# k and q of a linear attention: sixteen 128x512 matmuls a block replaced by seven products of 128x256 matmuls that share a PSUM bank

## The chip, the cores and the metric

The kernel runs on one core of a Trainium2 chip. The time is device microseconds of one execution, and the number compared is the median of several. TensorE is called PE below, its weight loads PEld, VectorE DVE, ScalarE ACT, GpSimd POOL and SyncE SP; "L217" is line 217 of the kernel before.

## What is computed

Two post-norm layers over x of (2, 1024, 512) in fp32, each with an attention and a feed-forward part, every part followed by a residual add and a layer norm. The change touches the first part alone:

```python
q = feature_map(proj(Wq))            # feature_map(y) = elu(y) + 1, 16 heads of 32
k = feature_map(proj(Wk))
v = proj(Wv)
kv = einsum('bhtd,bhte->bhde', k, v)
z = 1.0 / (einsum('bhtd,bhd->bht', q, k.sum(axis=2)) + 1e-06)
out = einsum('bhtd,bhde,bht->bhte', q, kv, z)
out = out.reshape(b, t, c) @ Wo.T
x = layernorm(x + out)
```

After it come a feed-forward part with weights unpacked from four bits, a gated linear attention in chunks, and a feed-forward part over the 512 best-ranked tokens of each batch.

## The kernel before, in words

The 2048 tokens are four blocks of 512 (two a batch), each of four tiles of 128 rows. x lies in SBUF twice: row by row (`x_t`, four tiles a block) and transposed (`xT`, three rooms that the blocks take in turn, loaded from a transposed copy in HBM). The four weight matrices lie in rooms A0 to A3 (`place_w`). PSUM is eight banks in two rings, "mm" (banks 0 to 3) and "acc" (4 to 7).

The first stage is the loop over `b` at L279. For each of the eight tiles of a batch, `project` (L214) makes k with four matmuls of 128x512, one per 128 input channels, into one bank; `elu1` (L266) turns it into elu + 1 with two ACT instructions and one DVE instruction that reads the bank (L269 to L271); POOL adds k up to `ksum` (L294, L296); and `add_xk` (L284) adds x'k of the tile to four accumulating banks with four matmuls (L286). For the very first block the four tiles are made side by side in all four "mm" banks (L303), because their operands are still arriving. So v is never formed: after the batch, Wv is applied to x'k (L338), the heads are cut out (L340), and Wo is applied (L347), which gives G, a 512x512 matrix. `ksum` is spread over the partitions with a matmul of ones (L330).

The second half of the loop makes q tile by tile in the same way (`new_q`), weighs it with z on DVE (`weigh`, L354 to L360: a product, a sum per head, an add, a reciprocal and a product), turns it with four transposes (L197) and ACT's copy (L365), multiplies it by G (`ao`, L217), adds it to x on DVE (L383) and takes the row statistics (L188, L189). The layer norm of a block runs on POOL (L181, L183). In the second batch the first block's x is meanwhile turned and split into two fp32r parts for the next stage (`split_quarter`, L211 and L212).

Between these steps stand 27 unpacking jobs (`unpack_some`): a load on SP, two integer instructions on DVE (L237, L238) and one conversion on ACT or DVE. Their loads use two buffers. The program order of the instructions on each engine is the order of the calls, moved a little by a scheduler; `tc.issue_after` ties an instruction behind another. Each engine works its queue in order.

The next stage (feed-forward, L471 for gate and up, L518 for the product with the unpacked matrix) starts with `gatep` at L471. L518 there already makes a product of block matrices from seven products of 128x256 matmuls.

Of the kernel before, what the change touches and what calls it, by code (L numbers as in the profile page):

```python
# [21 lines left out]
P = 128  # L22
B, T, C = 2, 1024, 512
NB = 4
# [49 lines left out]
def body(ctx: ExitStack, tc: tile.TileContext, a: dict, out: bass.AP):  # L74
# [8 lines left out]
    dram = ctx.enter_context(tc.tile_pool(name="dram", bufs=1, space=DRAM))  # L83


    rings, turn_of = {"mm": range(4), "acc": range(4, 8)}, {"mm": 0, "acc": 0}

    def bank(ring, name):
        i = rings[ring][turn_of[ring] % len(rings[ring])]
# [3 lines left out]
    def mm_bank(name):  # L93
        return bank("mm", name)
# [25 lines left out]
        return xtp.tile([P, KC, 512], dtype, tag=f"xT{i}", name=name)  # L120

    def new_xT(blk):
        t = xT_slot(blk % 3, f"x0T{blk}")
        return t, a["xT"][:, blk * 512 : (blk + 1) * 512].rearrange("(k p) t -> p k t", p=P)

    def load_xT(blk):
# [35 lines left out]
    wqk = cpool.tile([P, KC, 64], F32, name="wqk")  # L162

    def load_rest():
        xT[2] = load_xT(2)
        load_x(2)
        load_x(3)
        nc.sync.dma_start(out=gus, in_=a["gus"].rearrange("k (f p) -> (k f) p", p=P))
        nc.sync.dma_start(out=gw, in_=a["gw"])
        nc.sync.dma_start(out=b1, in_=a["b1"])  # L170
        nc.sync.dma_start(out=rb, in_=a["rb"].to_broadcast([P, 1]))
        nc.sync.dma_start(out=wqk[:, :, 0:32], in_=a["W1qT"].rearrange("(k p) o -> p k o", p=P))
        nc.sync.dma_start(out=wqk[:, :, 32:64], in_=a["W1kT"].rearrange("(k p) o -> p k o", p=P))
# [16 lines left out]

    last_turned = [None]

    def transposed(x, name):

        pt = mm_bank(name)
        for k in range(KC):
            ins = nc.tensor.transpose(pt[:, k * P : (k + 1) * P], x[:, k * P : (k + 1) * P], ident).ins  # L197
        last_turned[0] = ins
        return pt

    def split_tiles(blk):

        i, j = ((1, 1), (2, 0), (0, 2), (1, 1))[blk]
        hi = xT_slot(i, "x1Th", F32R)
        lo = wpool.tile([P, KC, 512], F32R, tag=f"A{j}", name="x1Tl")
        return hi, lo

    def split_quarter(parts, blk, i):
        hi, lo = (t[:, :, i * P : (i + 1) * P] for t in parts)
        pt = transposed(x_t[blk][:, i], "x1Tp").rearrange("p (k t) -> p k t", k=KC)  # L210
        nc.scalar.copy(hi, pt)  # L211
        nc.vector.tensor_sub(lo, pt, hi.bitcast(F32))  # L212

# [33 lines left out]
    def unpacking():  # L247
        n = 704
        for j in range(2 * I_FF // n):
            cut = slice(j * n, (j + 1) * n)  # L250
            for g in range(KC):
                yield wgu[:, g, cut], a["gu"][16 * g : 16 * (g + 1), cut], None, n
        for g in range(NI):
            yield wdn[:, g], a["dn"][16 * g : 16 * (g + 1), :], a["dns"][g : g + 1, :], C

    to_unpack = unpacking()
# [9 lines left out]
    def elu1(dst, ps):  # L266

        e = wk.tile([P, C], F32, tag="e", name="e")
        nc.scalar.activation(e, ps, AF.Relu, scale=-1.0)  # L269
        nc.scalar.activation(e, e, AF.Exp, scale=-1.0)  # L270
        anchor[0] = nc.vector.scalar_tensor_tensor(dst, ps, 0.0, e, ALU.max, ALU.add).ins  # L271

    ones = wk.tile([P, P], F32, name="ones", bufs=1)
    nc.gpsimd.memset(ones, 1.0)
    xk = wdn[:, NI - KC :]
    tile_of = lambda i: slice((i % 4) * P, (i % 4 + 1) * P)
    for b in range(B):  # L279
        acc = [acc_bank(f"xk{b}_{c}") for c in range(KC)]  # L280
        ksum = wk.tile([P, C], F32, tag="ksum", name="ksum", bufs=1)
        got = []

        def add_xk(i, k):  # L284
            for c in range(KC):
                nc.tensor.matmul(  # L286
                    acc[c], x_t[2 * b + i // 4][:, i % 4, c * P : (c + 1) * P], k, start=i == 0, stop=i == 7
                )

        def keys(i, kp):  # L290
            k = wk.tile([P, C], F32, tag="kq", name="k", bufs=5)
            elu1(k, kp)
            if i == 0:
                nc.gpsimd.tensor_copy(ksum, k)  # L294
            else:
                nc.gpsimd.tensor_add(ksum, ksum, k)  # L296
            return i, k

        if b == 0:
            first = [mm_bank("kp") for _ in range(4)]  # L300
            for k in range(KC):
                for i in range(4):
                    nc.tensor.matmul(first[i], xT[0][:, k, tile_of(i)], Wk[:, k], start=k == 0, stop=k == KC - 1)  # L303
            got = [keys(i, first[i]) for i in range(4)]
        for i in range(4 if b == 0 else 0, 8):
            kp = mm_bank("kp")
            project(kp, xT[2 * b + i // 4][:, :, tile_of(i)], Wk)
            for _ in range(max(1, len(got) - 2)):
                if got:
                    add_xk(*got.pop(0))  # L310
            got.append(keys(i, kp))
            unpack_some((i - 4 if i > 5 else 0) if b == 0 else 2 if i < 7 else 0)
            if b == 0 and i == 4:
                load_rest()
        for p in got:
            add_xk(*p)
        for c in range(KC):
            (nc.scalar.copy if c % 2 else nc.vector.tensor_copy)(xk[:, c], acc[c])

        def new_q(n):  # L320

            qp = mm_bank("qp")
            project(qp, xT[2 * b + n // 4][:, :, tile_of(n)], Wq)
            q = wk.tile([P, C], F32, tag="kq", name="q", bufs=5)
            elu1(q, qp)
            return q

        q = {n: new_q(n) for n in range(2)}
        sp_ = mm_bank("ksumb")
        nc.tensor.matmul(sp_, ones, ksum, start=True, stop=True)  # L330
        ks = wk.tile([P, C], F32, tag="ks", name="ks", bufs=1)
        nc.scalar.copy(ks, sp_)
        G = wk.tile([P, KC, C], F32, tag="G", name="G", bufs=1)
        vk = mm_bank("vk")
        for c in range(KC):
            cut = slice(c * P, (c + 1) * P)
            for k in range(KC):
                nc.tensor.matmul(vk[:, cut], Wv[:, k, cut], xk[:, k, cut], start=k == 0, stop=k == KC - 1)  # L338
        vkm = wk.tile([P, KC, P], F32, tag="vkm", name="vkm", bufs=1)
        nc.vector.tensor_mul(  # L340
            vkm,
            vk.rearrange("p (c d) -> p c d", c=KC),
            const("heads")[:, :P].unsqueeze(1).to_broadcast([P, KC, P]),
        )
        for c in range(KC):
            gp = acc_bank("gp")
            nc.tensor.matmul(gp, vkm[:, c], Wo[:, c], start=True, stop=True)  # L347
            (nc.scalar.copy if c % 2 else nc.vector.tensor_copy)(G[:, c], gp)

        def weigh(n):  # L350

            x = q[n]
            e = wk.tile([P, C], F32, tag="e", name="qk")
            nc.vector.tensor_mul(e, x, ks)  # L354
            z = sp.tile([P, 16], F32, tag="z", name="z", bufs=2)
            nc.vector.tensor_reduce(z, e.rearrange("p (h d) -> p h d", d=32), AX.X, ALU.add)
            nc.vector.tensor_scalar_add(z, z, 1e-6)
            nc.vector.reciprocal(z, z)
            x3 = x.rearrange("p (h d) -> p h d", d=32)
            return nc.vector.tensor_mul(x3, x3, z.unsqueeze(2).to_broadcast([P, 16, 32])).ins  # L360

        def turned(n):
            pt = transposed(q.pop(n), "qTp")
            t = wk.tile([P, KC, P], F32, tag="qT", name="qT")
            nc.scalar.copy(t.rearrange("p k t -> p (k t)"), pt)  # L365
            return t

        mv, qT = {}, {}
        for n in range(10):
            if n < 8:  # L370
                weighed = weigh(n)
            if n + 2 < 8:
                with tc.issue_after(weighed):
                    q[n + 2] = new_q(n + 2)
            if n >= 1 and n <= 8:
                i = n - 1
                blk = 2 * b + i // 4
                if i % 4 == 0:
                    mv = sp.tile([P, 4, 2], F32, tag="mv", name="mv")
                ao = acc_bank("ao")  # L380
                project(ao, qT.pop(i), G)
                x = x_t[blk][:, i % 4]
                nc.vector.tensor_add(x, ao, x)  # L383
                row_stats(mv[:, i % 4], x)
                if i == 7 and b == 1:
                    late = mv
                elif i % 4 == 3:
                    layernorm(x_t[blk], mv, by=nc.gpsimd)
                unpack_some(b or i % 2)
            if n < 8:  # L390
                qT[n] = turned(n)
            if b == 1 and n in (2, 3, 4, 5):
                if n == 2:
                    parts = split_tiles(0)
                split_quarter(parts, 0, n - 2)
            if b == 0 and n == 7:
                xT[3] = load_xT(3)
    unpack_some(1000)
    sg = wk.tile([KC * FG, P], F32, name="sg", bufs=1)
    nc.gpsimd.tensor_copy(sg, gus)  # L400
# [11 lines left out]

    free = iter([2, 1, 0] * 4)

    def xT_tile(name):
        return xT_slot(next(free), name)
# [24 lines left out]
    with tc.tile_pool(name="s2", bufs=1) as wk2:  # L443
# [43 lines left out]
        class Hidden:  # L487


            def __init__(self, blk):  # L490
                i, j = ((0, 2), (1, 1), (2, 0), (0, 2))[blk]
                self.rooms = xT_slot(i, "h"), place_w(j, "h"), extra[blk % 2]

            def chunk(self, f):
# [147 lines left out]
        for blk in range(NB):  # L642
# [45 lines left out]
            pieces = down(h, now.room)  # L688
            if blk > 0:
                old_steps = old.steps()  # L690
        Wog = place_w(1, "Wog")
        load_w(Wog, "WogT")
        rings["mm"], rings["acc"] = range(4), range(4, 8)
        with tc.issue_after(st):
# [9 lines left out]
        now.squares(range(4))  # L704
        now.power()
        ending = now.rest()
        W1o = place_w(2, "W1o")
    fp4.close()


# [713 lines left out]
```

## Time and profile before

| what | us |
|---|---|
| median of 3 runs | 1005.13 (1004.5 to 1005.25) |
| profiled execution, its own time | 1003.83 |
| its span, first to last instruction | 1002.0 |
| first matmul | 4.61 |
| first matmul of the next stage (L471) | 252.61 |
| busy PE, DVE, ACT, POOL over the span | 983.1, 644.6, 274.7, 299.2 |

The mean granted TensorE clock is 0.998 of full speed. The groups of the first stage that the change touches, each 128x512: a matmul pass (L217, L286) has a record of 592 ns, of which 429 ns pass until the next one; a weight load takes 190 ns; L269 takes 591 ns, L270 630, L271 690, L354 699, L356 682, L360 686, L383 686, L188 692, L365 584, and POOL's L296 1291 and L183 2211. To read it: a chain of waits shows which engine the end hangs on; an engine's busy share over the whole run says little about one stage, so the views are asked by stretch of time.

### The profile page before, as it was taken

To read this page: it belongs to the slowest core of one execution; us is meant where nothing else is said; L and a number is where in the kernel's file an instruction comes from. 1 tells how busy PE (TensorE), PEld (TensorE's weight loads), DVE (VectorE), ACT (ScalarE), POOL (GpSimd) and SP (SyncE) were. 2 spreads that over 40 slices of the span, in tenths; PEclk is the share of its full clock that TensorE was granted. 3 is DMA by queue.
4 is the path that set the end of the run, shared out by engine and by line. 5 is a ranking of instruction groups with operands and counts; after the bars stand their busy time and mean duration, and the time that the engine had idled before them with its cause. 6 is when DMAs were issued, how large, how long until landed. Compare 5 with 4: busy or idle time off the path is not lost.

```text
span 1002.0 us, 10997 instructions
## 1 busy us (share of the span) xinstructions
PE 983.1 (98%) x4061; PEld 708.8 (71%) x4061; DVE 644.6 (64%) x1233; ACT 274.7 (27%) x466; POOL 299.2 (30%) x277
## 2 busy tenths in 40 slices
PE   8999999999999999999999999999999999999996
PEld 3454444544788888888889765676778688888885
DVE  1236754476996576676664366656698795689644
ACT  2223222223463245245231333132220124220000
POOL 2100452004577536566557011201023002000022
PEclk9999999999999999999999999999999999999999
DMA  9611123100000000000011320000003402140011
GB/s 345 208 50 57 43 58 111 36 32 0 1 1 1 1 1 1 0 1 11 1 43 43 120 101 1 0 1 1 0 16 125 143 17 80 43 168 1 1 42 43
DMA packets 25689, 48.82 MB, mean 49 GB/s; under 512 B 4652, under 2 KB 6316, under 8 KB 25123
## 3 DMA queue, kind: packets, MB, share of 16 engines
q1 hardware_dynamic: 22995, 42.85, 13.0%
q0 software_dynamic: 1920, 4.22, 1.1%
q10 hardware_dynamic: 720, 1.05, 0.3%
q8 instruction: 32, 0.52, 0.2%
q14 instruction: 22, 0.18, 0.1%
HBM read 39.70 MB, written 10.52 MB: 50 GB/s over the span
## 4 chain that ended last, share of the span: by engine, by line
PE 84%; issue 8%; DVE 4%; POOL 2%; ACT 1%; DMA 0%; POOLq 0%; DVEq 0%; ACTq 0%
PE P L518 12%; PE yp L1168 9%; PE hp L1089 9%; PE upp L471 8%; PE gatep L471 8%; PE qp L217 5%; PE xk L286 5%; PE ao L217 5%; PE kp L217 4%; PE ao L972 3%; PE go L928 2%; PE lp L434 1%; PE kp L303 1%; PE P L527 1%; PE up L845 1%
## 5 line engine op out<-in xcount | busy, mean ns | idle before, releaser
L181 POOL TENSOR_TENSOR rs<-rs,table 128x4 f32<-128x4 f32 (+1 forms) x21 | 19.6, 936 | 324.2 <-DVE rs L180 323.9
L482 DVE SCALAR_TENSOR_TENSOR gate<-gatep,scale,gate 128x512 f32<-128x512 f32 x123 | 91.3, 742 | 7.3 <-PE gatep L471 6.7
L482 DVE SCALAR_TENSOR_TENSOR up<-upp,scale,up 128x512 f32<-128x512 f32 x112 | 83.0, 741 | 0.2
L471 PE MATMUL gatep<-x1Th,wgu 128*128 128x512 f32 x176 | 73.0, 415 | 0.0
L471 PE MATMUL upp<-x1Th,wgu 128*128 128x512 f32 x176 | 69.8, 397 | 0.0
L471 PE MATMUL gatep<-x1Tl,wgu 128*128 128x512 f32 x176 | 69.6, 395 | 0.0
L471 PE MATMUL upp<-x1Tl,wgu 128*128 128x512 f32 x176 | 69.5, 395 | 0.0
L671 POOL TENSOR_TENSOR h<-up,gate 128x512 f32<-128x512 f32 x30 | 38.6, 1286 | 78.3 <-ACT gate L670 73.3
L518 PE MATMUL P<-wdn,h 128*128 128x256 f32 x256 | 60.5, 379 | 0.0
L476 ACT ACTIVATE gate<-gatep,scale 128x512 f32<-128x512 f32 x41 | 28.3, 690 | 113.9 <-PE gatep L471 106.6
L217 PE MATMUL ao<-G,qT 128*128 128x512 f32 x128 | 57.5, 594 | 0.2 <-ACT qT L365 0.2
L217 PE MATMUL qp<-Wq,x0T 128*128 128x512 f32 x128 | 57.6, 592 | 0.0
L286 PE MATMUL xk<-k,x 128*128 128x512 f32 x128 | 56.7, 592 | 0.0
L972 PE MATMUL ao<-W1o,uT 128*128 128x512 f32 x128 | 55.6, 592 | 0.0
L518 PEld LDWEIGHTS P<-wdn,h 128*128 128x128 f32 x256 | 48.5, 190 | 6.7
L876 POOL TENSOR_TENSOR sum<-sum,sq 128x512 f32<-128x512 f32 x12 | 18.2, 1515 | 107.6 <-issue 83.7
L286 PEld LDWEIGHTS xk<-k,x 128*128 128x128 f32 x128 | 24.3, 190 | 30.6 <-issue 30.1
L217 PEld LDWEIGHTS ao<-G,qT 128*128 128x128 f32 x128 | 24.1, 190 | 30.4 <-issue 28.9
L972 PEld LDWEIGHTS ao<-W1o,uT 128*128 128x128 f32 x128 | 24.0, 190 | 28.7 <-issue 27.5
L271 DVE SCALAR_TENSOR_TENSOR k<-kp,e 128x512 f32<-128x512 f32 x16 | 11.0, 690 | 51.1 <-ACT e L270 47.2
L217 PE MATMUL kp<-Wk,x0T 128*128 128x512 f32 x96 | 43.4, 593 | 0.2 <-DVE k L271 0.2
L188 DVE BATCH_NORM_STATS2 st<-x 128x6 f32<-128x512 f32 x64 | 42.8, 682 | 0.8
(348 smaller groups left out, 2130.3 us busy)
## 6 DMA issues: line engine op xcount, KB each, us to landing
pk<-in_gu SPq DMA_DIRECT2D x16, 352.0 KB, 3.8
x<-in_x SPq DMA_DIRECT2D x4, 1024.0 KB, 12.7
w<-in_w SPq DMA_DIRECT2D x1, 4096.0 KB, 14.4
xs<-picked SPq DMA_DIRECT2D x4, 1024.0 KB, 5.2
out<-x SPq DMA_DIRECT2D x4, 1024.0 KB, 4.5
w<-in_w SPq DMA_DIRECT2D x4, 1024.0 KB, 6.6
x0T<-in_xT SPq DMA_DIRECT2D x3, 1024.0 KB, 8.7
pk<-in_dn SPq DMA_DIRECT2D x11, 256.0 KB, 3.6
```

What stands on the lines that cost most here:

```text
L188: nc.vector.bn_stats(st, x)
L217: nc.tensor.matmul(ps, lhs[:, k], w[:, k], start=start and k == 0, stop=stop and k == KC - 1)
L286: nc.tensor.matmul(acc[c], x_t[2 * b + i // 4][:, i % 4, c * P : (c + 1) * P], k, start=i == 0, stop=i == 7)
L471: ins = nc.tensor.matmul(ps, wgu[:, k, at * P : (at + 1) * P], x[:, k], start=x is parts[0], stop=x is parts[1]).ins
L476: nc.scalar.activation(acc, ps, AF.Copy, scale=s)
L482: last = nc.vector.scalar_tensor_tensor(acc, ps, s, acc, ALU.mult, ALU.add).ins
L518: last_p[0] = nc.tensor.matmul(cut, x(j)[:, r], w[:, j], start=j == 0, stop=j == NP - 1 and tail is None).ins
L671: hm = nc.gpsimd.tensor_mul(h.chunk(f), up, gate).ins
L928: nc.tensor.matmul(ps[:, 256 * m : 256 * m + 256], w[:, k, m], b[:, k, 256 * half : 256 * half + 256], start=k == 0, stop=k == KC - 1,)
L972: nc.tensor.matmul(ao[i], uT[blk][:, k, i * P : (i + 1) * P], W1o[:, k], start=n == 0, stop=n == 3)
L1089: nc.tensor.matmul(ps[:, 256 * j : 256 * j + 256], w[:, k, 2 * g + j], x[:, k], start=k == 0, stop=k == 1)
L1168: nc.tensor.matmul(ps[:, 256 * r : 256 * r + 256], x(r, j), w(j), start=j == 0, stop=j == NJ - 1)
```

## The change

For all blocks but the first, k is no longer made tile by tile. The block's transposed x (512 channels x 512 tokens) and the weights (512 x 512) are each taken as two by two blocks, and seven products of 256x256 blocks, each of four matmuls of 128x256, give the result (`by_seven`). Four sums of x blocks (S1 to S3, and S2 a second time) and, once per weight matrix, four sums of weight blocks (T1 to T4) are made on DVE. q is made so for all four blocks.

Four of the seven products (P1, S2 T2, S1 T1, S2 B22) go one after another into the same bank, "grow", and add up there. After each, ACT copies the bank as it stands into a part of the result, or elu reads it; the next of them is made when that is done. Two more (P7, A22 T4) share a second bank in the same way, read by DVE adds. P2 has a bank of its own. elu is applied to parts of 128x2x256, three of them from SBUF and one from PSUM.

What comes between the products is written out by hand: `run` takes a list of steps for each stop (`yield`). In the stops of k and q of one block stand x'k of the block before, the spreading of ksum, Wv and Wo, the transposes, ao and unpacking jobs of others. `behind()` ties each matmul group behind the one issued before it.

Rooms change with it: xT has two rooms instead of three for x (the third holds sums); the sums also use rw, b2, three slices of the not yet unpacked `wdn` and later Wk's room; x'k and G share one tile; the "mm" ring has banks 0 and 1 from the second block on, "grow" takes 2 and 3 in turn; transposes of q and of the split take "acc" banks. xT of block 2 is loaded after q of block 0 instead of early. In the later stages only the numbers of the rooms are exchanged.

```diff
+    def sums_of_weights(w, rooms):
+        B11, B12, B21, B22 = (w[:, 2 * e : 2 * e + 2, 256 * o : 256 * o + 256] for e in range(2) for o in range(2))
+        T1, T2, T4 = rooms
+        for dst, x, y in ((T1, B12, B11), (T2, B22, T1), (T4, B21, T2), (B12, B22, B12)):
+            nc.vector.tensor_sub(dst, x, y)
+        return T1, T2, B12, T4
+    def by_seven(x, w, T, rooms, pairs, ready):
...
+        def product(ps, a, b, first):
+            with behind():
+                for r in range(2):
+                    for k in range(2):
+                        ins = nc.tensor.matmul(
+                            ps[:, 256 * r : 256 * r + 256], a[:, k, r * P : (r + 1) * P], b[:, k],
+                            start=first and r == 0 and k == 0, stop=k == 1, skip_group_check=True,
+                        ).ins
+            last_pe[0] = ins
+            return ps.rearrange("p (r c) -> p r c", r=2)
+        nc.vector.tensor_add(S1, A21, A22)
+        nc.vector.tensor_sub(S2, S1, A11)
+        nc.vector.tensor_sub(S3, A11, A21)
...
+        grow = bank("sum", "grow")
+        p = product(grow, A11, B11, True)
+        nc.scalar.copy(c11, p)
+        yield
+        p2 = product(mm_bank("P2"), A12, B21, True)
+        nc.vector.tensor_add(c11, c11, p2)
+        elu1(c11, c11)
+        yield
+        product(grow, S2, T2, False)
+        nc.scalar.copy(c21, p)
+        side = mm_bank("P7")
+        p7 = product(side, S3, T3, True)
+        nc.vector.tensor_sub(S2, A12, S2)
+        yield
+        product(grow, S1, T1, False)
+        nc.scalar.copy(c22, p)
+        nc.vector.tensor_add(c22, c22, p7)
+        elu1(c22, c22)
+        yield
+        product(grow, S2, B22, False)
+        elu1(c12, p)
+        ready(0)
+        product(side, A22, T4, False)
+        nc.vector.tensor_add(c21, c21, p7)
+        elu1(c21, c21)
+        ready(1)
...
+    rings["mm"], rings["sum"] = (0, 1), (2, 3)
+    Ts = {"k": sums_of_weights(Wk, slices(Tk, 0, 3))}
+    for i in range(4):
+        elu1(pairs_of["k", 0][i // 2][:, i % 2], first[i])
...
+    for b in range(B):
+        i, j = 2 * b, 2 * b + 1
+        if b:
+            run(
+                k_products(i),
+                turns(1, 0, 1),
+                some_o(1, 0) + turns(1, 2) + job(1) + some_o(1, 1) + turns(1, 3) + job(1),
+                some_o(1, 2) + job(1), some_o(1, 3) + job(1), job(2),
+            )
+        run(k_products(j), [], some_xk(i, 0, 1) + job(2), some_xk(i, 2) + job(1), some_xk(i, 3) + job(1), job(1 + b))
+        if b == 0:
+            Ts["q"] = sums_of_weights(Wq, slices(wdn, 0, 3))
+        else:
...
+            Tq = place_w(1, "Tq")
+            for n in range(3):
+                nc.scalar.copy(Tq[:, n], wdn[:, n])
...
+        run(
+            q_products(i), [],
+            some_xk(j, 0, 1) + job(1), some_xk(j, 2) + step(spread_ksum, b) + job(1), some_xk(j, 3) + job(1 + b),
+        )
+        if b == 0:
+            xT[2] = load_xT(2)
+        split = [step(split_some, n) if b else [] for n in range(4)]
+        run(
+            q_products(j),
+            step(values, b),
+            turns(i, 0, 1) + job(1 - b),
+            step(G_rows, b) + split[0] + job(1 - b),
+            some_o(i, 0) + turns(i, 2) + split[1] + some_o(i, 1) + turns(i, 3) + job(1 - b),
+            some_o(i, 2) + split[2] + some_o(i, 3),
+        )
+        if b == 0:
+            xT[3] = load_xT(3)
+    for more in turns(3, 0, 1) + split[3] + some_o(3, 0) + turns(3, 2) + some_o(3, 1) + turns(3, 3) + some_o(3, 2, 3):
+        more()
```

The methods named in the lists (`add_xk`, `weigh`, `turned`, `add_o`, `spread_ksum`, `split_quarter`) do what their namesakes did before, for the tile given.

## The prediction, made before the changed kernel ran

> **What bounds the kernel now.** I read the page first, then the busy time by stretch, the chain of waits, and last the groups and the order in time.
>
> ```profile
> span 1002.0 us, 10997 instructions
> PE 983.1 (98%) x4061; PEld 708.8 (71%) x4061; DVE 644.6 (64%) x1233; ACT 274.7 (27%) x466; POOL 299.2 (30%) x277
> ...
> PE 84%; issue 8%; DVE 4%; POOL 2%; ACT 1%; DMA 0%; POOLq 0%; DVEq 0%; ACTq 0%
> ```
>
> PE carries the span. The changed stage is the first quarter; its two ends by stretch (columns: stretch, length, then busy us of PE, PEld, DVE, ACT, POOL, then granted clock, DMA share, GB/s):
>
> ```profile
> 118.00:184.00 66.00, 66.00 (x160) 29.38 (x159) 35.60 (x65) 17.46 (x28) 23.94 (x15) 1.00 0.31 88
> 184.00:202.00 18.00, 18.00 (x67) 9.77 (x66) 7.47 (x14) 4.68 (x8) 0.00 (x0) 1.00 0.00 1
> 202.00:253.00 51.00, 50.84 (x156) 24.92 (x154) 35.03 (x75) 15.31 (x27) 10.15 (x5) 1.00 0.05 16
> ```
>
> PE has no holes at full clock; DVE is 54% to 69% busy, ACT has room. So PE time taken out of this stage shortens the run, as far as DVE can follow. The chain (start, us, what) gives the prices:
>
> ```profile
> 4.61 13.84 PE kp L303 x28
> 18.46 0.60 ACT e L269
> 19.06 0.53 ACT e L270
> 19.61 0.70 DVE k L271
> 20.36 3.70 PE kp L217 x8
> ...
> 30.92 3.43 PE kp L217 x8
> ...
> 303.47 6.47 PE P L518 x30
> ```
>
> Each matmul has two records (fp32 takes two passes). Four 128x512 matmuls take 3.43 us, 0.429 a record. L518, in the next stage, already runs the new form, 128x256 on 128x128 weights: 6.47/30 = 0.216 a record.
>
> **The products.** A block of 512 tokens was 16 matmuls of 128x512: 4 x 3.43 = 13.7 us. It becomes 28 of 128x256: 56 x 0.216 = 12.1. Seven blocks change (k of blocks 1 to 3, q of 0 to 3; k of block 0 stays): 7 x 1.64 = **11.5 us less PE**. x'k, ao, the transposes, L330, L338 and L347 keep their number and size and only move.
>
> Here a rule speaks against the change. The Trainium skill ("TensorE: Matmul & The Clock Gate", section Back-to-back issue gap) says that in a stream of weight load and matmul pairs the spacing depends on both, and gives 81 ns at 128 columns and 131 at 512. Halfway in columns between, an estimate from that page, 256 would cost about 98 ns, 0.75 of a 512: a block would be 28 x 0.75 = 21 old matmuls against 16, seven blocks 30 us dearer. The row says 0.216/0.429 = 0.50, because the 190 ns weight load of L518 still fits under its 216 ns pass. I take the row; it is the same shape.
>
> **Price 1, the start.** Block 0's k still fills four banks and ends where it did (same loads, same L303). Before, the next matmul needs the first bank and starts at 20.36, behind one DVE k. Now the growing bank is the third of those four, so PE waits for the third elu. That one is in the trace:
>
> ```profile
> 20.40 0.60 ACT L269 ACTIVATE e<-kp 128x512 f32<-128x512 f32 x1 [0.30 <-DVE k L271]
> ...
> 21.03 0.63 ACT L270 ACTIVATE e<-e 128x512 f32<-128x512 f32 x1
> ...
> 21.69 0.69 DVE L271 SCALAR_TENSOR_TENSOR k<-kp,e 128x512 f32<-128x512 f32 x1 [0.79 <-ACT e L270]
> ```
>
> It ends at 22.38, so PE starts at 22.42: **+2.1 us**. The four sums of Wk and three of xT stand ahead of these elus in DVE's queue. They cost nothing: DVE is idle to 19.61, and block 1's xT, issued at 5.61 with 8.7 us to landing, is there at 14.3, plus three sums = 16.4. Had it landed at the 14.2 us that another xT took, the start would slip by about 2 more. Wq's four sums (2.4 us of DVE) come behind the third elu and delay only the first c11, which has 20 us.
>
> **Price 2, DVE and the stops.** Each of the seven blocks adds four sums of x and three adds of a product on DVE, three bank copies on ACT (7 x 3 x 0.59 = 12 us, in ACT's idle time). The elus keep their number; three of four read SBUF now. 49 DVE instructions more, at what spacing?
>
> ```profile
> 232.68 0.68 DVE L383 TENSOR_TENSOR x<-ao,x 128x512 f32<-128x512 f32 x1
> 233.28 0.68 DVE L360 TENSOR_TENSOR q<-q,z 128x512 f32<-128x512 f32 x1
> 233.88 0.69 DVE L188 BATCH_NORM_STATS2 st<-x 128x6 f32<-128x512 f32 x1
> 234.48 0.67 DVE L212 TENSOR_TENSOR x1Tl<-x1Tp,x1Th 128x512 fp32r<-128x512 f32 x1
> ...
> 235.35 0.68 DVE L354 TENSOR_TENSOR qk<-q,ks 128x512 f32<-128x512 f32 x1
> 236.07 0.69 DVE L356 TENSOR_REDUCE z<-qk 128x16 f32<-128x512 f32 x1
> ```
>
> Independent instructions follow each other in 0.60 us, though one takes 0.68; where one needs its forerunner it is 0.72. A 128x16 one takes 0.10 to 0.15 between others. 49 x 0.60 = 29 us more DVE in 230, so it holds PE only where it comes in a burst: the weighing of q.
>
> Inside a block the waits that the change adds (each product into the growing bank waits for ACT's copy of the one before; behind it in PE's queue stands all else) are covered: the copy is ready 0.2 + 0.59 us after its product, and between stand another product (1.73) and mostly x'k or ao (3.43). Without that cover each would show about 0.8 us.
>
> At q of blocks 0 and 2 the transposes of q follow the last product by 1.73 (side product) + 1.73 (next P1) + 3.57 (vk) + 1.73 (P2) = 8.8 us. The chain behind the growing bank's last product is 0.2 hand-over, 0.60 + 0.63 ACT and hand-overs, so DVE starts at 1.5; elu, p7 add, two mul, two reduce, a sum of x, elu, mul, mul, with a next qk between, are 11 at 0.60, and some small ones: both tiles done at 8.7. Just covered, 0 to 1 us. Block 1 has two ao on top, 10.3 us.
>
> The tail (q of block 3) has no next block. Clock from the end of the growing bank's last product. PE: side 1.73, ao 3.43, transposes 0.44, ao 3.43, two q transposes 0.88, pg 0.08: at 9.99 it wants the last transposes for the split. Their bank is the one that the split before them used, freed by its DVE subtraction (L212). That stands in DVE's queue behind 16 full instructions (elu, p7 add, four of weighing, two mul, elu, x add, four of weighing, stats, mul) and nine small ones: 1.5 + 16 x 0.60 + 1.1 + its own 0.69 = 12.9. PE stalls 12.95 - 9.99 = 2.96, and all of block 3's ao and the next stage are queued behind. The next ao needs a bank that DVE frees 0.75 later: **+3.7 us**. The 0.2 us that ao waits for ACT there now goes.
>
> In the middle the 0.4 us that the transposes wait for DVE at 117.60 goes (block 2's first product stands there, ao beside it); I allow 0.5 for new small waits, between 0 and 1.5.
>
> The skill also bears on DVE ("SBUF — State Buffer", Who interferes with whom): a DVE instruction with two SBUF inputs contends with a GpSimd one that reads SBUF, and the second blocks for the whole of the first. That is what the 28 x sums and 21 of the elus become.
>
> ```profile
> L354 DVE TENSOR_TENSOR qk<-q,ks x16: 656/680/1096, 70.7 to 239.0; 128x512 f32<-128x512 f32 x16
> ```
>
> L354 has two SBUF inputs. At 118.07 it took 1.10 us beside GpSimd's normalization; at 238.95, beside the same 2.1 us instructions, 0.69. One in 16 paid 0.4. By the rule, with GpSimd 50 us busy of 233, about 10 of 49 would wait 1 us: 10 us of DVE, mostly in the k stretches, and perhaps 3.5 on PE. By the row it is 49 x 0.03 = 1.3 us of DVE, within my allowance; in the tail GpSimd is idle. I take the row.
>
> **Queues.** xT of block 2 moves from the early loads to behind q of block 0, as block 3's sits behind q of block 1. PE frees the room at about 75, SP issues then, and with 8.7 us it lands at 84, with 14.2 at 89; DVE first reads it at about 89 to 92. Covered; if not, DVE's queue stops there and PE about 3 us later. Unpacking loads behind it on SP have two buffers and the same cover. GpSimd keeps its work. The three copies of the weight sums (ACT, 1.8 us) run in x'k stops.
>
> **The sum.** -11.5 + 2.1 + (3.7 - 0.2) + (0.5 - 0.4) = -5.8 us. The following stages are PE-bound with rooms only renamed, so it reaches the end. The profiled execution took 1003.83 us with 1002.0 span: 998.0 and 996.2. The median of runs is 1005.13, 1.3 above it: **999.3 us**. About 0.2% (2 us) is what a measurement here can tell from no change.
>
> **Rivals.**
> *No tail stall* (14%): DVE drains faster, or records overstate its hand-overs. -11.5 - 0.6 + 2.1 + 0.5 = -9.5: 995.6. Against: the tail needs 3 us less from 11.
> *GpSimd lock* (14%): as the rule above, -5.8 + 3.5: 1002.8. For: the 1.10 us. Against: the 0.69.
> *DVE becomes the bound, slower* (9%): one mechanism, DVE spacing in the q chains. At 0.75 instead of 0.60 (small ones 0.08 more) the tail is 3.7 + 16 x 0.15 + 9 x 0.08 = 6.8, blocks 0 and 2 lose their 0.5 slack and 1.4 each, and the G copies, x adds and transposes queued behind lose about 1 at each of four places: 2.1 + 6.8 + 2.8 + 4 - 0.6 = 15.1 against 11.5, +3.6: 1008.7. It decides from about 0.71 on; most of this work is dependent, at 0.72, which speaks for it, but pairs of tiles alternate in the queue, which gives 0.60.
> *The products don't pay* (3%): the skill's 98 ns, up to 1035. Against: L518.
>
> My forecast has 60%, 997 to 1001.5. Faster by over 0.2% (below 1003.1): forecast, no tail, and half of the lock, 0.81; slower: DVE's bound and the products, 0.12; 0.07 between. The range leaves out the products, the slower case and the fastest tip: 995.5 to 1004.
>
> **What would show it.** Right: grow and P products at 0.216 a record, 12.1 us a block; first grow at 22.4; one PE gap of about 3 us before the last split transposes, released by DVE, and one under 1 us at the next ao; the gate products start at 252.61 - 5.8, about 246.8. Wrong: gaps ahead of grow products released by ACT; DVE idle under 10% from q of block 2 on; 128x256 records over 0.23 apart; the gate products early but the end not.

## The result, and the profile after

| | before | after |
|---|---|---|
| median (lowest to highest) of 6 runs, us | 1004.68 (1003.83 to 1005.25) | 999.14 (997.57 to 1001.8) |
| ratio, 95% interval | | 0.995 [0.9933, 0.9968] |
| profiled execution: own time, span | 1003.83, 1002.0 | 998.07, 996.3 |
| mean granted clock | 0.998 | 0.996 |
| first matmul; first one after block 0's k | 4.61; 20.36 | 4.57; 22.84 |
| first gate product, and from there to the end | 252.61; 749.4 | 246.72; 749.5 |

The forecast was 999.3. The whole gain lies ahead of the gate products. The runs of after lie three times as far apart as those of before, which asks for a reason as well. ("After" is the changed kernel; "before", "after" and the names of the runs also stand for their profiles.)

The page of the kernel after, the same three lines:

```profile
span 996.3 us, 11402 instructions
PE 972.5 (98%) x4229; PEld 741.8 (74%) x4229; DVE 681.1 (68%) x1290; ACT 288.7 (29%) x490; POOL 302.6 (30%) x277
...
PE 83%; issue 8%; DVE 5%; POOL 2%; ACT 2%; DMA 0%; POOLq 0%; DVEq 0%; ACTq 0%
```

PE lost 10.6 us of busy time with 168 records more; the span lost only 5.7. The difference has to be idle PE. Busy time by stretch (stretch, length, then busy us of PE, PEld, DVE, ACT and POOL, granted clock, DMA share, GB/s):

```profile
20.50:62.00 41.50, 39.20 (x135) 25.48 (x135) 24.32 (x36) 16.52 (x27) 10.81 (x9) 1.00 0.58 182
62.00:118.00 56.00, 56.00 (x224) 37.38 (x223) 42.35 (x88) 21.61 (x36) 1.57 (x2) 1.00 0.23 71
118.00:184.00 66.00, 66.00 (x228) 42.42 (x227) 46.41 (x75) 21.20 (x35) 30.35 (x17) 1.00 0.26 79
184.00:202.00 18.00, 18.00 (x97) 14.96 (x96) 17.40 (x38) 8.14 (x14) 0.00 (x0) 1.00 0.00 0
202.00:247.00 45.00, 41.74 (x138) 22.68 (x136) 26.61 (x55) 12.67 (x23) 9.28 (x5) 0.96 0.00 1
```

From 62 to 202 PE has no hole, though DVE is 97% busy in the 18 us of the fourth row. All idle time is in the first and the last stretch, and in the last the mean granted clock is 0.96; in before it stays at 1.00 from 20 us on until the last 5 us of the program. The start, in the chain:

```profile
4.57 14.28 PE kp L467 x28
...
20.02 0.70 DVE k L272
...
22.10 0.70 DVE k L272
22.80 0.04 issue
22.84 1.99 PE grow L311 x8
24.84 1.73 PE P L311 x8
```

The first growing product waits for the third elu, as forecast. A product then takes 1.73 us for eight records, 0.216 each. The tail, PE in order of time (start, us, instructions in a row, and in brackets the idle time with its releaser):

```profile
226.87 0.24 PE L552 MATMUL pg<-table,sg 88*128 88x88 f32 x1
229.74 0.66 PE L196 MATMUL x1Tp<-table,x 128*128 128x128 f32 x4 [2.63 <-DVE x1Tl L211]
231.03 5.08 PE L440 MATMUL ao<-G,qT 128*128 128x512 f32 x8 [0.63 <-ACT x1Th L210]
235.94 0.60 PE L196 MATMUL qTp<-table,pair 128*128 128x128 f32 x4
236.38 3.60 PE L440 MATMUL ao<-G,qT 128*128 128x512 f32 x8
```

Two waits in the places named, 2.63 and 0.63 us. But the ao behind them takes 5.08 us where the next one takes 3.60. The same time in stretches shows why:

```profile
227.03:230.45 3.42, 0.73 (x6) 0.42 (x4) 3.42 (x11) 2.31 (x6) 0.00 (x0) 1.00 0.00 0
230.45:233.86 3.41, 2.83 (x4) 1.31 (x5) 2.07 (x5) 0.57 (x1) 1.02 (x1) 0.50 0.00 0
233.86:237.27 3.41, 3.41 (x13) 1.69 (x12) 1.09 (x2) 0.59 (x1) 3.31 (x3) 1.00 0.00 0
```

The granted clock is 0.50 for 3.41 us behind the hole, and 1.00 again after that. Such a stretch is called a low stretch below. The price of the tail therefore has a part that the prediction lacks. Theory for the experiments: products 11.5 us cheaper, less one wait at each end, and each wait can bring a lowered clock on top. Rivals: the waits are not what costs (DVE or the GpSimd lock holds PE generally), or the products gain less and something unseen makes it up.

### The profile page after: what moved, and what is told of

Read it like the earlier page. It is cut to its first block, busy times and chain, and to the rows that moved or that the text cites. A ratio compares the mean times of both kernels' runs of the same rounds, so it can differ in the third digit from the quotient of the medians.

```text
span 996.3 us, 11402 instructions
## 1 busy us (share of the span) xinstructions
PE 972.5 (98%) x4229; PEld 741.8 (74%) x4229; DVE 681.1 (68%) x1290; ACT 288.7 (29%) x490; POOL 302.6 (30%) x277
## 4 chain that ended last, share of the span: by engine, by line
PE 83%; issue 8%; DVE 5%; POOL 2%; ACT 2%; DMA 0%; POOLq 0%; DVEq 0%; ACTq 0%
PE P L668 12%; PE yp L1318 9%; PE hp L1239 9%; PE gatep L621 8%; PE upp L621 8%; PE xk L362 6%; PE ao L440 5%; PE grow L311 5%; PE P L311 3%; PE ao L1122 3%; PE go L1078 2%; PE kp L467 1%; PE lp L584 1%; PE P L677 1%; PE up L995 1%
## 5 line engine op out<-in xcount | busy, mean ns | idle before, releaser
L362 PE MATMUL xk<-pair,x 128*128 128x512 f32 x96 | 42.7, 592 | 0.0
L621 PEld LDWEIGHTS upp<-x1Th,wgu 128*128 128x128 f32 x176 | 33.0, 188 | 9.3 <-DVE up L632 1.1
L621 PEld LDWEIGHTS gatep<-x1Th,wgu 128*128 128x128 f32 x176 | 33.1, 188 | 7.7 <-PE x1Tp L196 0.3
L621 PEld LDWEIGHTS upp<-x1Tl,wgu 128*128 128x128 f32 x176 | 33.1, 188 | 7.5
L621 PEld LDWEIGHTS gatep<-x1Tl,wgu 128*128 128x128 f32 x176 | 33.1, 188 | 7.2 <-issue 0.2
```

The lines of the kernel that those rows point to most:

```text
L362: ins = nc.tensor.matmul(acc_of[b][c], x_t[blk][:, i, c * P : (c + 1) * P], pairs_of["k", blk][i // 2][:, i % 2], start=blk % 2 == 0 and i ...
L621: ins = nc.tensor.matmul(ps, wgu[:, k, at * P : (at + 1) * P], x[:, k], start=x is parts[0], stop=x is parts[1]).ins
```

## The experiments

**The tail's bank.** The last two split transposes take a bank of the "mm" ring, so they no longer wait for the subtraction that frees theirs.

```diff
-                split_quarter(parts, 0, i, acc_bank)
+                split_quarter(parts, 0, i, mm_bank if i > 1 else acc_bank)
```

> The last two split transposes take a bank of the other ring (0, 1), so nothing at the end of q of block 3 waits for a bank that DVE has to free. In the changed kernel PE stood idle there 2.63 and 0.63 us, and the ao matmuls after it took 5.08 us in place of 3.43 at a granted clock of 0.53 to 0.61. Theory (a bank wait, and a lower clock because PE stood still): both waits and the slow ao go, -2.6 -0.6 -1.6 = -4.9 us, gate products at about 241.8, run 994.3; the runs lie closer together, with a mean clock of 0.998 in all. Rival (DVE's load at the end is what binds, the bank only shows it): PE waits at the q transposes or at the next ao instead, gain under 1.5 us.

Measured 993.04 us (992.94 to 995.93), ratio to before 0.9884 [0.9868, 0.9901]: 6.1 below the median of after, where 4.9 was expected. The tail's waits are gone, and the ao there takes 3.67 us. One of the four runs, the profiled one, took 2.9 us more than the others, and shows a reason; PE at the start:

```profile
23.80 3.57 PE L311 MATMUL grow<-Wk,x0T 128*128 128x256 f32 x8 [2.30 <-DVE k L272]
27.16 2.05 PE L311 MATMUL P<-Wk,x0T 128*128 128x256 f32 x8
```

The same product after the same 2.30 us wait took 1.99 us in the profile of after. Here the clock fell (0.50 from 24.06 to 27.47), there it did not. So the start's hole lowers the clock in some executions. That makes 1.7 of the 2.9 us, half of the 3.41; block 0's k also ended late in this run (21.51, in after 20.55), and when it ended in the other three is not on record. The mean clock tells the low stretches of runs without a profile, since one takes 0.0017 off it (1.7 of 996 us; an estimate, since the program's end takes another 0.0017 to 0.003 in the profiles): the other three runs here have 0.998 and so none. Every run of after has at least one: three have a mean of 0.996, which makes one low stretch (997.57 to 998.71 us), one 0.995, one or two (999.58), and two 0.993, three (1001.75 and 1001.8). That is how far the runs of after spread.

**The start's banks.** The first growing product gets the bank that block 0's first tile frees.

```diff
-    rings["mm"], rings["sum"] = (0, 1), (2, 3)
+    rings["mm"], rings["sum"] = (2, 3), (0, 1)
```

> The growing banks are 0 and 1, the side banks 2 and 3, so the first product after block 0's k needs the first elu and not the third. Theory: first grow starts near 20.8 and not 22.84; P2 then waits some 0.3 us for the third elu; gain 1.7 to 2.0 us, run 997.3. Rival (PE is held by something later in the first x'k anyway, or DVE falls behind by as much): grow early, but the gap reappears before the first x'k or S2 T2, gain under 0.5 us.

Measured 995.26 us (994.93 to 997.91), ratio 0.9905 [0.9889, 0.9922]: 3.9 below the median of after, more than expected. The wait at the start is 0.21 us and the tail is untouched:

```profile
21.33 1.99 PE L311 MATMUL grow<-Wk,x0T 128*128 128x256 f32 x8 [0.21 <-DVE k L272]
...
228.59 1.12 PE L196 MATMUL x1Tp<-table,x 128*128 128x128 f32 x4 [2.63 <-DVE x1Tl L211]
229.88 6.24 PE L440 MATMUL ao<-G,qT 128*128 128x512 f32 x8 [0.17 <-DVE x L448]
```

The wait is worth 2.1. The rest of the 3.9 is the clock: the other three runs have a mean of 0.998, so no low stretch at all, although the tail's wait is untouched by the edit. The profiled run has two in a row in the tail (6.24 and 1.12 us instead of 5.08 and 0.66), and took 2.4 to 3.0 us more than the other three. So the hole in the tail does not always lower the clock either.

**Both.** The two edits together.

> Both changes of banks together: growing banks 0 and 1 from the start, the last two split transposes in the other ring. Theory (two PE gaps of 2.3 and 2.6 us, each of which can also lower the clock for about 3 us): relative to the tail change alone (993.0) the start gap of 2.1 us and the chance of a clock drop there (1.7 us in some runs) go: 990 to 991, granted clock 0.998, runs within 1 us of each other. Rival (gains share a cause and don't add): 992 to 993.

Measured 991.48 us (991.24 to 992.21), ratio 0.987 [0.9853, 0.9886], between the two expectations; the runs agree within 1 us again, at a mean clock of 0.997 to 0.998. It beats both kernels. All waits of PE from 20 us to the gate products (us in total, times, longest):

```profile
PE grow L311 <- DVE k L272: 0.2, 1, 0.2
```

That also answers where the other 7.7 us of after went: about 1.6 for the start's wait (the step from the tail's edit to both; the rows had 2.1, and why it is less stays open), 3.3 for the tail's two waits, and the remainder of 2.8 for the clock. The mean clocks agree: one to three low stretches a run, on average 1.7 or 1.8, at 1.7 us each are about 3.0.

**Work in the hole.** To separate the wait from the clock: three 128x512 matmuls of ones with ksum, whose results nobody reads, stand ahead of the last split transposes of after. They delay nothing while PE would wait anyway.

```diff
+    def warm():
+        with behind():
+            for _ in range(3):
+                last_pe[0] = nc.tensor.matmul(mm_bank("warm"), ones, ksum_of[1], start=True, stop=True).ins
...
-    for more in turns(3, 0, 1) + split[3] + ...
+    for more in turns(3, 0, 1) + [warm] + split[3] + ...
```

> Three matmuls of 128x512 that nobody reads (ones by ksum) are put where PE waits for the last split transposes; the wait for the bank stays. Theory that the idle PE lowers its clock: the granted clock stays at 1.00 and the next ao takes 3.43 us in place of 5.08, while the transposes start where they did (229.7): about -1.6 us, run 997.5. Rival (ao is slow for its operands or for what ACT and DVE do beside it): ao keeps 5.08 us, time as the changed kernel or up to 0.5 more.

Measured 998.81 us (996.39 to 998.97), ratio 0.9934 [0.9918, 0.9951]: not told apart from after in the total. The rows of PE decide it:

```profile
228.83 2.74 PE L548 MATMUL warm<-ksum,ones 128*128 128x512 f32 x6
231.41 0.24 PE L557 MATMUL pg<-table,sg 88*128 88x88 f32 x1
231.71 0.66 PE L196 MATMUL x1Tp<-table,x 128*128 128x128 f32 x4
...
233.37 3.60 PE L440 MATMUL ao<-G,qT 128*128 128x512 f32 x8
```

With PE at work the same ao takes 3.60 us, so the 5.08 was the clock and not the memory, the bank or the trace. The total did not show it because three of the four runs still have one low stretch by their mean clock (0.996); in the profiled one it lies at the start (the first growing product took 3.54 us). The fourth has 0.998 and took 996.39 us.

**Eight products.** The plain block scheme: eight products of the same 128x256 matmuls, two per bank, elu on the bank. It leaves out all sums of x and weights, the bank copies and the adds of products; what it computes is the same.

```diff
+        def whole(ring, name, x1, w1, x2, w2, c):
+            ps = bank(ring, name)
+            p = product(ps, x1, w1, True)
+            product(ps, x2, w2, False)
+            elu1(c, p)
+
+        whole("sum", "c11p", A11, B11, A12, B21, c11)
...
```

> Order, stops and rooms of the changed kernel, but each block is made from the eight plain block products (32 matmuls of 128x256, 13.8 us), two to a bank, elu reading the bank; no sums of x or weights, no copies of a bank. Theory (the gain is the missing eighth product, the new order is worth little): 7 blocks x 1.73 = +12.1 us of PE, at the end one DVE add less: run 1009 to 1011, slower than the kernel before by 5 us. Rival (the hand-written order removes waits of the kernel before and is what gains): 1000 to 1004.

Measured 1014.26 us (1012.32 to 1015.98), ratio 1.0099 [1.008, 1.0118]: 15.1 more than after, 3 more than seven products account for, and above the 1009 to 1011 expected. The weighing now comes only after the block's last product, so the transposes of q wait for DVE (1.0 us in two waits in the middle, 0.8 in the tail), and the tail's ao takes 6.03 us. So it is not a clean price of a product; the next one is.

**One product twice.** Both bank edits, and P2 made twice into its own bank in each of the seven blocks; the second overwrites the first with the same numbers.

```diff
-        p2 = product(mm_bank("P2"), A12, B21, True)
+        p2_bank = mm_bank("P2")
+        product(p2_bank, A12, B21, True)
+        p2 = product(p2_bank, A12, B21, True)
```

> Both bank edits, and in each of the seven blocks the second product (P2) is made twice, one after the other, into the same bank; the second overwrites the first with the same numbers. This prices one product of four 128x256 matmuls where it stands. Theory (PE carries the stage, 0.216 us a record): 7 x 1.73 = 12.1 us on top of the 991.5 of the two bank edits: 1003.6, less up to 0.2 for a wait that it covers. Rival (the products are partly hidden behind DVE, whose work stays the same): clearly less than 12, below 1001. Other rival (the weight loads show at this width): over 1005.

Measured 1003.88 us (1002.93 to 1004.47, 12 runs), ratio 0.9994 [0.9985, 1.0002]: 12.4 more than with both bank edits, and level with the kernel before. The row of the first doubled product:

```profile
23.71 3.72 PE L311 MATMUL P<-Wk,x0T 128*128 128x256 f32 x16
```

A product made twice shows in full: 12.4 us for seven, where the records ask for 12.1. PE sets the pace of this stage, and its weight loads (190 ns) don't show beside 128x256 matmuls (216 ns a record).

**Twice the sums.** Both bank edits, and S1, S2 and S3 made twice on DVE, 21 instructions more.

```diff
-        nc.vector.tensor_add(S1, A21, A22)
-        nc.vector.tensor_sub(S2, S1, A11)
-        nc.vector.tensor_sub(S3, A11, A21)
+        for _ in range(2):
+            nc.vector.tensor_add(S1, A21, A22)
+            nc.vector.tensor_sub(S2, S1, A11)
+            nc.vector.tensor_sub(S3, A11, A21)
```

> Both banks changed, and S1, S2, S3 of every block are made twice on DVE, into the same rooms: 21 more DVE instructions, 13 us of DVE. Theory (DVE has room outside the tail, and the q transposes of blocks 0 and 2 have 0.5 to 1.5 us of it): +0 to +1.5 us on the run with both banks. Rival (DVE already near the bound in the q stretches, deciding at a spacing of 0.71): +4 us or more.

Measured 996.17 us (995.69 to 996.56), ratio 0.9915 [0.9899, 0.9932]: 4.7 over both bank edits, which is what the rival of a generally bound DVE asked for. But the waits lie otherwise. Those of PE from 20 us on, and the place:

```profile
PE grow L311 <- DVE rw L320: 2.7, 1, 2.7
PE grow L311 <- DVE k L272: 0.2, 1, 0.2
```

```profile
195.17 1.04 PE L196 MATMUL qTp<-table,pair 128*128 128x128 f32 x8
198.96 3.53 PE L311 MATMUL grow<-Tq,rw 128*128 128x256 f32 x8 [2.75 <-DVE rw L320]
202.33 1.89 PE L311 MATMUL P<-Wq,b 128*128 128x256 f32 x8
```

It is one wait, in q of block 3, where the second S2 stands in DVE's queue among the weighing of block 2 and behind two unpacking jobs. 2.75 us of it are the wait, and 1.6 the lowered clock once more (3.53 against 1.89). Both expectations missed: mine for thinking that DVE had room everywhere, the rival for thinking that it had none.

**Twice the sums in six blocks.** To test that reading: the same, but in q of block 3 they are made once.

```diff
-        for _ in range(2):
+        by_seven.calls = getattr(by_seven, "calls", 0) + 1
+        for _ in range(2 if by_seven.calls < 7 else 1):
```

> Both bank edits, and S1 to S3 made twice on DVE in six of the seven blocks, but once in q of block 3, the block where the earlier run with all seven doubled lost its time. Theory (DVE has the room for them everywhere but at that one place): 991.5 to 992.2, and no wait of a growing product for DVE over 0.5 us. Rival (the loss belongs to DVE's load as a whole and moves to the next place): 994 or more, with a wait elsewhere.

Measured 991.8 us (991.49 to 992.17), ratio 0.9876 [0.9859, 0.9892]: 0.3 over both bank edits, for 18 of the 21 instructions. The loss was that one place.

**The sums on GpSimd.** Both bank edits, and S1 to S3 made by GpSimd, so that it reads SBUF while DVE works.

```diff
-        nc.vector.tensor_add(S1, A21, A22)
-        nc.vector.tensor_sub(S2, S1, A11)
-        nc.vector.tensor_sub(S3, A11, A21)
+        nc.gpsimd.tensor_add(S1, A21, A22)
+        nc.gpsimd.tensor_sub(S2, S1, A11)
+        nc.gpsimd.tensor_sub(S3, A11, A21)
```

> Both banks changed, and S1, S2, S3 of every block on GpSimd in place of DVE (28 us of GpSimd more, 13 us of DVE less). Theory that the two engines hardly hinder each other: time as with both banks, within 0.7 us, DVE's two-input instructions beside GpSimd keep 0.69 us. Rival (the lock of the Trainium skill's SBUF page): DVE instructions with two SBUF inputs beside GpSimd's sums grow to over 1 us, GpSimd's own stretch too, and PE waits for DVE or GpSimd: +2 us or more.

Measured 992.13 us (991.68 to 992.82), ratio 0.9876 [0.986, 0.9893]: 0.65 over both bank edits. DVE's two-input instructions did not all keep their 0.69 us. The clearest pair, DVE's elu of two SBUF inputs beside one of GpSimd's sums, each from its engine's rows:

```profile
85.16 1.67 POOL L320 TENSOR_TENSOR b<-x0T 128x512 f32<-128x512 f32 x1 [11.75 <-PE P L311]
...
85.62 1.75 DVE L272 SCALAR_TENSOR_TENSOR pair<-pair,e 128x512 f32<-128x512 f32 x1
```

1.75 us instead of 0.68. Nine DVE instructions of the stage took 1.15 to 1.76 us beside GpSimd here, and seven took 1.02 to 1.75 with the bank edits alone. PE waited for none of them.

**All other work first.** Both bank edits, and the work of all stops of a block stands ahead of its seven products instead of between them.

```diff
-        others = list(others)
-        for _ in products:
-            for step in others.pop(0):
-                step()
         for more in others:
             for step in more:
                 step()
+        for _ in products:
+            pass
```

> Both banks changed, and the steps of each stop (x'k, transposes, ao and the rest) are all put ahead of the block's products, which then follow one another with nothing between. Theory (the stops' work covers the waits): about 0.85 us at the third product into the growing bank, 7 times; 3.4 us at the q transposes of blocks 0 and 2 and about 7 at those of blocks 1 and 3, where only one product is left as cover, and some clock drops of 1.7 to 3.3 us: +25 to +33 us, 1015 to 1024. Rival (waits of a product for a copy of its bank are free, as PE has other banks' work in its queue): +5 or less.

Measured 1022.74 us (1022.19 to 1025.19), ratio 1.0187 [1.017, 1.0204]: 31 over both bank edits. PE's waits:

```profile
PE qTp L196 <- DVE pair L401: 9.4, 4, 4.5
PE grow L311 <- ACT pair L338: 4.7, 7, 0.7
PE xk L362 <- DVE pair L272: 3.6, 3, 2.3
PE ao L440 <- DVE G L426: 1.2, 1, 1.2
```

With smaller ones they come to 21.7 us. The profile has three low stretches (two from 120.27, one from 253.39), which take some 4.6 us of PE's work, an estimate: 9.2 us of records at half clock. Some 5 us are not assigned. One line is the price of a growing bank by itself: without work between, each of the seven blocks waits 0.67 us for ACT's third copy of the growing bank (L338), ahead of the last growing product. With the work between, none does.

## Why the prediction was right, step by step

The time (999.3 against 999.14) is right, and so is the mechanism: the gate products start at 246.72, forecast about 246.8. That it fits so closely is luck: terms of the sum were off in both directions and cancelled.

*The products*: 11.5 us. Right: 0.216 us a record in every block of the trace, and a product more costs 12.4 (forecast 12.1). The rule of the Trainium skill, 30 us dearer, falls to the row. (256 columns are a third of the way from 128 to 512, not half; the 98 ns are right for a third.)

*The start*: forecast +2.1 with the first growing product at 22.42; it came at 22.84, +2.5. The wait itself is as forecast, 2.30 us instead of 0.21; block 0's k, which the change leaves alone, ended at 20.55 instead of 20.14 in this execution (20.08 to 21.51 in the profiles). Of what this wait was to cost, the edit gave back 1.6 to 3.9, depending on the low stretches of the runs compared.

*The tail*: forecast 2.96 and 0.75, found 2.63 and 0.63, in both places and with the releaser of the first as forecast. The second was put down to a bank that DVE frees, while its row names ACT's copy of the transposed x. The bank is right, as the same ao in the run with the start's edit shows (the first row is from after, the others from that run):

```profile
230.20 0.68 DVE L448 TENSOR_TENSOR x<-ao,x 128x512 f32<-128x512 f32 x1
...
229.05 0.68 DVE L448 TENSOR_TENSOR x<-ao,x 128x512 f32<-128x512 f32 x1
...
229.74 0.59 ACT L210 CAST x1Th<-x1Tp 128x512 fp32r<-128x512 f32 x1 [1.54 <-PE x1Tp L196]
```

There ao started at 229.88, while ACT's copy was still running. In both runs it started 0.15 us after the DVE add that reads its bank (230.88 to 231.03, 229.73 to 229.88); in after the copy happened to end at the same time. The step "+3.7" was mis-sized nonetheless: the hole lowered the clock, and ao took 1.5 us more (5.08 against the 3.60 of the next). With that the tail cost 4.7.

*The middle*: "+0.5 - 0.4", so +0.1 in all; found about -1.3. The -0.4 came, the allowance of +0.5 was not needed, and two gains were not foreseen. No wait of PE between 23 and 226 us; the copy waits are covered as argued, and uncovered they are 0.67 (about 0.8 forecast). In after the wait of before at 117.60 is gone (about 0.5 with its restart), and also 0.5 us in Wo's products (3.43 instead of 3.69, twice) and about 0.3 of slower restarts.

So the measured sum: -11.5 - 0.5 - 0.5 - 0.3 + 2.5 + 3.3 + 1.5 = -5.5, where the profiled executions differ by 5.8; 0.3 us stays open. The forecast -5.8 lacked the +1.5 and about 1.2 of small gains. It is the sum of the profiled run alone: by the mean clock two or three of the six runs of after have more low stretches than this one has.

*Queues*: x of block 2 came in time, as forecast: PE has no hole there.

*The lock* (14%): the row of before that carried the weighing against it,

```profile
L395 DVE TENSOR_TENSOR qk<-pair,ksum x16: 631/683/687, 76.9 to 225.6; 128x512 f32<-128x512 f32 x16
```

now shows no long one in 16 (its columns are least, median, most, in ns). Other instructions were held instead: in after two sums of Wq beside GpSimd's ksum took 1.16 and 1.75 us, and four of the 21 elus that read SBUF took 1.02 to 1.37. Against the usual 0.68 to 0.69 that is 3.4 us of DVE more, between the 1.3 that the prediction took from the row and the 10 of the rule, with no wait of PE behind them. The trace agrees with the skill ("SBUF — State Buffer", Who interferes with whom) that such pairs can block each other; as a rule for what a stage costs it overstates it here.

*DVE as the bound* (9%): not here. The sign I had named for it, DVE idle under 10% from q of block 2 on, did appear for a while (97% busy from 184 to 202) without any wait of PE, so it was a bad sign. But the bound is nearer than I thought. One extra burst of three sums in the wrong place is 4.4 us, in the other six places nothing.

*No tail stall* (14%, 995.6): did not happen; the bank edit makes it happen, at 993.0.

## To carry to other kernels

Price a wait of the engine that carries the span with the wait and with what its standing still does to the clock afterwards: here 1.5 to 3 us on top of 2.3 to 2.75. When results grow in a shared bank, ask at each end of the stage who freed that bank last, since inside the stage other work hides the copy and at the ends nothing does. Ask also how a hole can be split or filled: the same wait of 2.30 us brought the lowered clock or not, by how it lay on a grid of 3.41 us (next section). And before calling an engine free by its busy share, look for the burst that stands ahead of the one result that is waited for.

## What the runs showed of the hardware

In all twelve profiles the granted clock changes only at times that lie a whole number of steps of 3.41 us apart (in after at 230.45, 233.86 and 991.62: 1 and 222 steps), and in a low stretch it is 0.50. On this grid one sees why the same hole lowered the clock in one execution and not in the next. PE is idle for 2.30 us at the start in both kernels below; the first two rows are after, the others the run with the tail's edit:

```profile
18.82:22.23 3.41, 1.73 (x5) 0.42 (x3) 1.42 (x3) 3.03 (x6) 1.37 (x2) 1.00 1.04 386
22.23:25.65 3.42, 2.81 (x13) 2.50 (x14) 3.42 (x5) 1.54 (x3) 3.14 (x3) 1.00 1.05 389
...
20.64:24.06 3.42, 1.12 (x4) 0.30 (x3) 2.29 (x4) 3.05 (x6) 2.04 (x3) 1.00 1.04 385
24.06:27.47 3.41, 3.41 (x9) 2.70 (x9) 3.41 (x4) 0.17 (x2) 3.01 (x2) 0.50 1.05 387
```

In after the hole lies across two steps, 1.68 us in one and 0.61 in the other, and the clock stays. In the other run it lies within one, and the next step is at half clock. Counted over the twelve profiles from 11 us on, each of the 20 steps at full clock in which PE was idle for 2.05 us or more was followed by a low one (eight of them in the first stage, the others at the program's end), and none of those with 1.72 us or less was. No profile has one between, so the boundary is known no closer. In the first stage the low clock lasted one step in five of the eight cases and two in three. Where it lasted two, PE had been idle for 0.55 to 1.00 us in the first of them; where it lasted one, for 0 to 0.58. These overlap, so what decides it stays open.

The Trainium skill ("TensorE: Matmul & The Clock Gate", Why this matters for your kernels) warns of gaps over about 3 us; here shorter ones did it: 2.30 us (start), 2.63 (tail), 2.75 (twice the sums), and 2.11 with one of 0.82 shortly ahead (eight products).
